# Four graph layers on one core: the hubs' weighted values summed over places by identity products on TensorE

## Chip, core and metric

The kernel runs on one core of a Trainium2 chip. The metric is the device time of one execution in microseconds (us). A core has TensorE (PE), VectorE (DVE), ScalarE (ACT), GpSimd (POOL) and DMA queues, one of them issued by SyncE (SP). Each engine takes its instructions from its own queue in order, and engines wait for one another by semaphores. PE reads SBUF and writes PSUM.

## What is computed

Sixteen graphs of 1024 nodes with 64 channels go through four layers, each with a residual and a layer norm:

```python
x = _layernorm(x + _L0_gnn_ref(x, adj, nodemask, ...), axis=-1)   # quantiles over neighbours, then an MLP
x = _layernorm(x + _L1_gnn_ref(x, adj, ...), axis=-1)             # adj @ (x W)
x = _layernorm(x + _L2_gnn_ref(x, adj, ...), axis=-1)             # attention plus adj
x = _layernorm(x + _L3_gnn_ref(x, adj, nodemask, ...), axis=-1)   # quantiles over neighbours, then an MLP
```

The first and the last take, for every node and channel, the values of its neighbours (some edges are dropped by a rule of rank), sort them, and add the quantiles at 0.25, 0.5 and 0.75 with weights 0.25, 0.5 and 0.25, interpolated between two places:

```python
pos = jnp.clip(tau * (mf - 1.0), 0.0)
q = gather(lo) * (1.0 - frac) + gather(hi) * frac
agg = agg + wt * q
```

That is the same as a weighted sum of the sorted list over its places, where at most six weights of a list are not zero. The kernel computes it so.

## The kernel before

**Layers.** The two quantile layers of each of 16 batches make 32 "layers" (n = 0 to 31), worked in a pipeline. Seven streams are generators that yield instructions: graph (adjacency, dilation, ranks of nodes by degree, lists of neighbours), turn, pick, weight, middle (MLP, layer norms, the two middle layers), sort and fetch. The nodes are ordered by degree. The 128 with the longest lists are the hubs; the others are "short" and are sorted in three groups.

**The hubs' path of one layer.** The fetch stream issues 50 indirect DMAs on POOL that gather neighbours' rows into hrows (8 buffers of two gathers each). The turn stream (from L1488) transposes each with an identity product on PE into the PSUM tile "turned" (one buffer), and ACT copies from there into two SBUF tiles cols[0] and cols[1], each 128 partitions x 32 places x 55 columns (half a list's chunk in each column, channels on partitions). The sort stream runs long_lists (from L1616) on DVE: a network over the 32 places of each column, merges of columns, each step from cols to a spare tile or back. Then summed (L1673) multiplies a block by the fp16 weights hw and adds the 32 places by five halving additions (16, 8, 4, 2, 1 places), and small operations add the columns that belong to one list into tot. An event "block" says that a block is done, "hubdone" that both are. The turn stream waits for hubdone, turns tot with two products, ACT copies the result to hagg, and POOL puts it into DRAM. Only then does the turn stream begin the next layer's transposes.

A few columns of block 0 (the first SPLIT = 9) hold two half lists; there the upper 16 places are summed apart into "more" and added to another list's total.

**The short rows' path.** 85 gathers a layer on POOL into rows, a network on DVE, a weighting on ACT, sums over places by identity products on PE ("picked"), and puts.

**Order of the instructions.** give_out (L259) decides it while the program is built. It keeps a planned time for each engine and tile, takes from the heads of all streams the instruction that could start first (the earlier stream when equal), and puts it at the end of its engine's queue. The costs come from Queue.times (L214): a cost, in which the engine is held, and a lateness until others see the result. Every instruction so placed is recorded by one closure, so the profile gives nearly all of them line L211, and groups are told apart by tiles and shapes. A Wait in a stream holds the stream in the plan only; on the chip waits come from the tiles that are read and written.

Of the kernel before, what the change touches and what calls it, by code (L numbers as in the profile page):

```python
# [9 lines left out]
F32 = mybir.dt.float32  # L10
# [7 lines left out]
ALU = mybir.AluOpType  # L18
AX = mybir.AxisListType
# [19 lines left out]
HC = 55  # L39
# [3 lines left out]
HUB_RUNS = ((0, 18, 9, 32, 1, False), (9, 10, 25, 0, 1, False), (34, 10, 8, 32, 1, False), (42, 35, 13, 0, 1, False),  # L43
            (55, 0, 1, 0, 8, True), (63, 1, 1, 0, 5, True), (68, 2, 2, 0, 4, True), (76, 4, 6, 0, 2, True),
            (88, 4, 6, 64, 1, True), (94, 48, 16, 0, 1, True))
# [13 lines left out]
SPLIT = 9  # L59
UPPER = (0, 27, SPLIT, 16, 1, False)  # L60
CH = 32
# [125 lines left out]
class Queue:  # L187
# [26 lines left out]
    def times(self, name, args, sizes, halves, psum, accum):  # L214
        n, half = max(sizes), all(halves)
        if self.engine == "V":
            rate = 1.9 if name == "tensor_reduce" and n > 256 and not psum else 1.1
            if name in ("tensor_tensor", "tensor_mul", "tensor_add", "tensor_sub") and half and not psum:
                rate = 0.52
            elif name in ("tensor_scalar", "tensor_copy", "memset") and not psum:  # L220
                rate = 0.26 if half else 0.52
            return 75 + rate * n, 120
        if name == "dma_start":
            return 100, 3000 + 128 * sizes[0] * 4 / 100.0
        if self.engine == "A":
            return 110 + 1.0 * sizes[0] + 200 * accum, 150
        if self.engine == "T":
            cols = sizes[0]
            if halves[1]:
                return max(45, 0.5 * cols), 250  # L230
            return (220 if name == "transpose" else 2 * max(200, 1.25 * cols)), 250
        if self.engine == "G":
            return (1435, 4000) if name == "indirect_dma_start" else (1000, 200)
        raise ValueError(name)
# [601 lines left out]
def listed_path(ctx: ExitStack, tc: tile.TileContext, x, adj, nodemask,  # L836
# [5 lines left out]
    P = 128  # L842
# [7 lines left out]
    V, A, T, G = nc.vector, nc.scalar, nc.tensor, nc.gpsimd  # L850
# [10 lines left out]
    ident = const.tile([P, P], F32, name="ident")  # L861
# [12 lines left out]
    run = const.tile([P, P], F16, name="run")  # L874
# [52 lines left out]
    for (first, places), (end, fewer) in zip(HUB_CAPS, HUB_CAPS[1:] + ((64, 0),)):  # L927
        more = const.tile([P, 1], F32, name=f"more{first}")
# [5 lines left out]
    for k in (1, 2, 3):  # L934
        s = const.tile([P, 7, MOST], F32, name=f"shifted{k}")
# [56 lines left out]
    with tc.tile_pool(name="wps", bufs=2, space=PSUM) as wps:  # L992
        pt = wps.tile([C, C], F32, name="pt")
# [18 lines left out]
    qp = pool("qp")  # L1012
    small = {"g": pool("small_g", 2), "t": pool("small_t", 2)}
    psm = pool("psm", space=PSUM)
    psh = pool("psh", space=PSUM)
# [11 lines left out]
    V, A, T, G, D = (Queue(c, e) for c, e in zip("VATGD", (nc.vector, nc.scalar, nc.tensor, nc.gpsimd, nc.sync)))  # L1027
    events = set()
# [459 lines left out]
    def turn_stream():  # L1488
        for n, (l, b) in enumerate(layers):
            k = batches[b]  # L1490
            yield Wait("hidx", b)
            k.cols = [None, None]
            for g in range(0, NG, 4):
                pt = psh.tile([P, 4 * P], F32, name="turned")
                for i in range(g, min(g + 4, NG)):
                    yield Wait("h", n, i)
                    yield T.transpose(pt[:, (i - g) * P:(i - g + 1) * P], k.hrows[i].rearrange("p h c -> p (h c)"),
                                      ident).after(6000)
                events.add(("turned", n, g // 4))
                first, end = g * GC, min((g + 4) * GC, GW)  # L1500
                by_slot = pt.rearrange("p (c s) -> p s c", s=CH)
                for i in range(2):
                    c0, c1 = max(first, i * GB), min(end, (i + 1) * GB)
                    if c0 < c1 and c0 == i * GB:
                        if n:
                            yield Wait("block", n - 1, i)
                        k.cols[i] = qp.tile([P, CH, HC], F32, name=f"cols{i}")
                        for c, m, s0, places in EMPTY:
                            if c // HC == i:
                                yield A.copy(k.cols[i][:, s0:s0 + places, c - i * HC:c - i * HC + m],  # L1510
                                             bigs[:, :places * m].rearrange("p (s c) -> p s c", c=m))
                    if c0 < c1:
                        runs = [(0, CH, c, n_ * chunks, to, 0) for c, _, n_, _, chunks, to in WHOLE]
                        runs += [(q * PART, PART, c, n_, to, s0) for q, c, n_, _, _, to, s0 in PARTS]
                        for at, places, c, m, to, s0 in joined(runs):
                            a, b = max(c0, c), min(c1, c + m)
                            if a < b:
                                d = to + a - c - i * HC
                                yield A.copy(k.cols[i][:, s0:s0 + places, d:d + b - a],
                                             by_slot[:, at:at + places, a - first:b - first])  # L1520
                    if c0 < c1 and c1 == (i + 1) * GB:
                        events.add(("cols", n, i))
            yield Wait("hubdone", n)
            pt = psh.tile([P, C], F32, name="turned")
            for h in range(2):
                rs = slice(h * C, (h + 1) * C)
                yield T.matmul(pt[rs], k.tot[rs], ident[rs, rs], start=True, stop=True)
            k.hagg = qp.tile([P, C], F32, name="hagg", bufs=2)
            yield A.copy(k.hagg, pt)
            events.add(("hagg", n))  # L1530
# [23 lines left out]
    def sort_stream():  # L1554
        for n, (l, b) in enumerate(layers):
            k = batches[b]
            yield Wait("cols", n, 0)
            if n > 1:
                yield Wait("put", n - 2)
            k.tot = qp.tile([P, 64], F32, name="tot", bufs=2)  # L1560
            yield from long_lists(n, k)
            events.add(("hubdone", n))
            for q, (t0, ntiles, places) in enumerate(TILE_GROUPS):
                yield Wait("rows", n, q)
                for t, s, m in PAIRS:
                    if t0 - 1 <= t < t0 - 1 + ntiles:
                        yield V.memset(k.rows[l, q][P // 2:, s:s + 2 * m, t - t0 + 1, :], BIG)
                yield from network((k.rows[l, q], spare((places, ntiles, C))), plans[q], C)
                events.add(("net", n, q))
# [46 lines left out]
    def long_lists(n, k):  # L1616
# [56 lines left out]
        def summed(block, spans):  # L1673

            yield Wait("hw", n, block)
            w = bufs[side[spans[0][0]]][block]
            for c0, c1 in spans:
                assert len(set(side[c0:c1])) == 1
                cols = slice(c0 % HC, c0 % HC + c1 - c0)
                yield V.tensor_tensor(w[:, :, cols], bufs[side[c0]][block][:, :, cols], k.hw[block][:, :, cols], ALU.mult)  # L1680
            half = CH // 2
            skip = 0 if block else SPLIT
            while half:
                yield V.tensor_add(w[:, :half, skip:], w[:, :half, skip:], w[:, half:2 * half, skip:])
                half //= 2
                skip = 0
            for c0, first, lists, p0, chunks, by_list in sorted(HUB_RUNS, key=lambda run: run[3]):
                if c0 // HC == block:
                    v = w[:, 0, c0 % HC:c0 % HC + lists * chunks]
                    v = v.rearrange("p (l k) -> p l k" if by_list else "p (k l) -> p l k", k=chunks)  # L1690
                    mine = k.tot[:, first:first + lists]
                    if p0:
                        yield V.tensor_add(mine, mine, v[:, :, 0])
                    elif chunks == 1:
                        yield V.tensor_copy(mine, v[:, :, 0])
                    elif chunks == 2:
                        yield V.tensor_add(mine, v[:, :, 0], v[:, :, 1])
                    else:
                        yield V.tensor_reduce(mine, v, AX.X, ALU.add)
            if not block:  # L1700
                more = qp.tile([P, SPLIT - 1], F32, name="more")
                yield V.tensor_reduce(more, w[:, CH // 2:, :SPLIT - 1].rearrange("p s c -> p c s"), AX.X, ALU.add)
                mine = k.tot[:, UPPER[1]:UPPER[1] + SPLIT - 1]
                yield V.tensor_add(mine, mine, more)
            events.add(("block", n, block))

        yield from first(0)

# [243 lines left out]
```

## Time and profile before

| what | value |
|---|---|
| median of 3 runs | 7255.36 us (7244.06 to 7256.55) |
| the profiled execution | 7250.51 us, its span 7248.6 us |
| granted TensorE clock, mean | 0.646 |
| POOL gathers and puts | 4544, mean 1.1 us, with about 0.3 us of issue between two |
| DVE: hub sort steps, spare<-cols | 1792 instructions, 1016.1 us |
| DVE: hub sort steps, cols<-spare | 1632 instructions, 1017.1 us |
| PE: picked (sums over places of short rows) | 432.1 us of 832 products from rows |
| PE waiting for tot ("turned <- DVE tot") | 236.3 us in 17 waits, longest 80.5 |

Busy time is what the engine's own records cover; times of waits are idle times of an engine, put down to what ended them last. A group's line gives busy time, mean time of one and the idle time before it. On PE instructions overlap in the pipeline, so that the busy time over the count tells what one more costs, and the mean of one tells how long it is under way. Where stretches are given, they run from the span's start.

### The profile page before, as it was taken

How to read it: one execution, taken by the hardware profiler on the slowest of the kernel's cores; microseconds unless marked ns; L12 is line 12 of the kernel's file. 1: busy time of each engine (PE TensorE's matmuls, PEld its weight loads, DVE VectorE, ACT ScalarE, POOL GpSimd, SP SyncE). 2: the span in 40 equal slices, each digit the busy share in tenths (PEclk: the TensorE clock that was granted, in tenths of full speed). 3: DMA queues.
4: the chain of work that ended last, by engine and by line, in shares of the span. 5: the costliest groups of instructions: out<-in, count | busy, mean ns of one | idle time of the engine just before them, and what ended most of it. 6: DMA issues, size and time to landing. Idle time of an engine off the chain costs nothing. (4 is left out here: it accounts for less than half of the span.)

```text
span 7248.6 us, 75571 instructions
## 1 busy us (share of the span) xinstructions
PE 4032.2 (56%) x20163; PEld 2014.5 (28%) x20163; DVE 6433.9 (89%) x16469; ACT 2468.9 (34%) x8066; POOL 5144.3 (71%) x4606
## 2 busy tenths in 40 slices
PE   4358664847475564646647465574756647262541
PEld 3223232323232322223223232322223223121211
DVE  4878798999999999989989899898989989999876
ACT  3324333343333434234342333423234342222231
POOL 2653777777776777767777776777767677777764
PEclk7557676757566665766666566665666766565565
DMA  2231413141323223231231322323231232121211
GB/s 68 68 100 34 127 35 107 52 113 50 87 64 88 61 58 85 68 88 49 59 102 53 88 57 66 86 56 89 68 87 49 59 99 56 45 71 42 57 41 23
DMA packets 515446, 498.74 MB, mean 69 GB/s; under 512 B 203712, under 2 KB 351424, under 8 KB 514752
## 3 DMA queue, kind: packets, MB, share of 16 engines
q1 hardware_dynamic: 218048, 262.03, 11.9%
q0 software_dynamic: 146432, 150.24, 9.5%
q10 hardware_dynamic: 150528, 81.54, 3.8%
q8 instruction: 164, 2.69, 0.1%
q14 instruction: 274, 2.24, 0.1%
HBM read 393.02 MB, written 102.50 MB: 68 GB/s over the span
## 5 line engine op out<-in xcount | busy, mean ns | idle before, releaser
L211 POOL DMA_INDIRECT rows<-table,idx x2720 | 3064.2, 1127 | 829.9 <-issue 790.6
L211 POOL DMA_INDIRECT hrows<-table,hidx x1600 | 1781.5, 1113 | 905.1 <-issue 373.3
L211 DVE TENSOR_TENSOR spare<-cols 128x192 f32<-128x192 f32 (+15 forms) x1792 | 1016.1, 599 | 57.4 <-ACT cols L211 40.5
L211 DVE TENSOR_TENSOR cols<-spare 128x528 f32<-128x528 f32 (+14 forms) x1632 | 1017.1, 652 | 11.1
L211 PE MATMUL picked<-rows,ident 128*128 128x512 f32 (+5 forms) x832 | 432.1, 628 | 399.8 <-ACT rows L211 375.9
L211 ACT ACTIVATE rows<-rows,wt 128x64 f32<-128x64 f32 x1856 | 499.3, 348 | 207.8 <-DVE rows L211 183.6
L211 DVE TENSOR_TENSOR spare<-rows 128x128 f32<-128x128 f32 (+8 forms) x1056 | 539.2, 541 | 31.7 <-DMA rows<-table,idx 17.8
L211 POOL DMA_INDIRECT sums<-agg,node x224 | 256.1, 1143 | 313.9 <-ACT agg L211 213.0
L211 DVE TENSOR_TENSOR rows<-spare 128x512 f32<-128x512 f32 (+8 forms) x864 | 451.0, 551 | 1.9
L211 PE MATMUL two<-ident,a 128*128 128x128 f32 x1024 | 239.6, 411 | 364.9 <-DMA a<-in_adj_dram 271.7
L211 DVE TENSOR_TENSOR spare<-spare 128x64 f32<-128x64 f32 (+11 forms) x640 | 399.4, 624 | 16.5
L211 PE MATMUL one<-xt,wt 64*128 64x512 f32 x512 | 374.1, 1024 | 36.1 <-DVE top L211 35.6
L211 ACT ACTIVATE v<-two,before 128x128 f16<-128x128 f32 x1024 | 278.8, 385 | 310.7 <-DVE before L211 179.4
L211 PE MATMUL pi<-hot,numbers 128*32 128x200 f16 x4096 | 241.5, 327 | 250.9 <-DVE hot L211 248.6
L211 DVE TENSOR_TENSOR rows<-rows,spare 128x128 f32<-128x128 f32 (+4 forms) x1088 | 347.6, 328 | 17.5
L211 PE MATMUL po<-at,y 128*64 128x512 f32 x512 | 285.2, 752 | 138.0 <-DMA at<-adjt 94.7
L211 PE MATMUL turned<-ident,hrows 128*128 128x128 f32 x800 | 229.7, 358 | 228.6 <-DMA hrows<-table,hidx 209.2
L211 PE MATMUL po<-at,x 128*64 128x512 f32 x512 | 277.5, 780 | 129.6 <-DMA at<-adjt 117.9
L211 PE MATMUL pu<-e,x 128*65 128x512 f32 x512 | 311.0, 698 | 62.3 <-ACT e L211 62.3
L211 ACT COPY at<-two 128x1024 f32<-128x1024 f32 x128 | 129.5, 1012 | 612.7 <-PE two L211 562.0
L211 PEld LDWEIGHTS picked<-rows,ident 128*128 128x128 f32 x832 | 182.5, 272 | 523.7 <-ACT rows L211 487.7
L211 DVE TENSOR_SCALAR hot<-slot 128x1600 f16<-128x1600 f16 x512 | 300.4, 590 | 25.1 <-PE pi L211 22.8
(273 smaller groups left out, 9052.7 us busy)
## 6 DMA issues: line engine op xcount, KB each, us to landing
at<-adjt SPq DMA_DIRECT2D x512, 256.0 KB
a<-in_adj_dram SPq DMA_DIRECT2D x128, 512.0 KB
adjt<-at ACTq DMA_DIRECT2D x128, 512.0 KB
rows<-table,idx POOLq DMA_INDIRECT x2720
hw<-hwt SPq DMA_DIRECT2D x64, 440.0 KB
hrows<-table,hidx POOLq DMA_INDIRECT x1600
hwt<-ho ACTq DMA_DIRECT2D x64, 220.0 KB
ag<-sums SPq DMA_DIRECT2D x32, 256.0 KB
```

The lines of the kernel that those rows point to most:

```text
L211: return Step(lambda: f(*args, **kw), self.engine, cost, late, reads, writes, "dma" in name)
```

## The change

The five halving additions of each block leave summed. It now only multiplies, always into cols, and gives an event "weighed". The turn stream waits for it and adds the places on PE: 32 products of the fp32 identity with the 55 columns of one place each, all into one PSUM tile; for the last 16 places of block 0 the first 9 columns are left out. The small operations that make tot stay on DVE, but read PSUM and stand in the turn stream; a sum of two columns is a reduction now. "more" is reduced from cols as before. Beside that, the planner's costs for ACT and PE are changed.

```diff
         if self.engine == "A":
-            return 110 + 1.0 * sizes[0] + 200 * accum, 150
+            first = 60 if name == "copy" else 180
+            return first + 0.82 * sizes[0] + 100 * accum, 150
         if self.engine == "T":
             cols = sizes[0]
             if halves[1]:
-                return max(45, 0.5 * cols), 250
-            return (220 if name == "transpose" else 2 * max(200, 1.25 * cols)), 250
+                return max(45, (0.3 if args[0].shape[0] <= 32 else 0.85) * cols), 250
+            return max(170, 240 if name == "transpose" else 1.4 * cols), 250
...
-            yield Wait("hubdone", n)
+            k.tot = qp.tile([P, 64], F32, name="tot", bufs=2)
+            for block in range(2):
+                yield Wait("weighed", n, block)
+                w = k.cols[block]
+                pt = psh.tile([P, HC], F32, name="turned")
+                for s in range(CH):
+                    skip = 0 if block or s < CH // 2 else SPLIT
+                    yield T.matmul(pt[:, skip:], ident, w[:, s, skip:], start=(s == 0), stop=(s == CH - 1))
+                for c0, first, lists, p0, chunks, by_list in sorted(HUB_RUNS, key=lambda run: run[3]):
+                    if c0 // HC == block:
+                        v = pt[:, c0 % HC:c0 % HC + lists * chunks]
...
+                        if p0:
+                            yield V.tensor_add(mine, mine, v[:, :, 0])
+                        elif chunks == 1:
+                            yield V.tensor_copy(mine, v[:, :, 0])
+                        else:
+                            yield V.tensor_reduce(mine, v, AX.X, ALU.add)
...
+                events.add(("block", n, block))
...
             yield Wait("hw", n, block)
-            w = bufs[side[spans[0][0]]][block]
+            w = k.cols[block]
...
-            half = CH // 2
-            skip = 0 if block else SPLIT
-            while half:
-                yield V.tensor_add(w[:, :half, skip:], w[:, :half, skip:], w[:, half:2 * half, skip:])
-                half //= 2
-                skip = 0
...
-            events.add(("block", n, block))
+            events.add(("weighed", n, block))
```

Two more lines go: in the sort stream, layer n no longer waits in the plan for the puts of layer n - 2 before tot is made, and hubdone is gone.

More of the change, by code (lines that the diff above doesn't have):

```diff
@@ L1522, in turn_stream @@
                         events.add(("cols", n, i))
-            yield Wait("hubdone", n)
+            k.tot = qp.tile([P, 64], F32, name="tot", bufs=2)
[9 more added lines that the diff above has]
+                        v = pt[:, c0 % HC:c0 % HC + lists * chunks]
+                        v = v.rearrange("p (l k) -> p l k" if by_list else "p (k l) -> p l k", k=chunks)
+                        mine = k.tot[:, first:first + lists]
+                        if p0:
[4 more added lines that the diff above has]
+                            yield V.tensor_reduce(mine, v, AX.X, ALU.add)
+                if not block:
+                    more = qp.tile([P, SPLIT - 1], F32, name="more")
+                    yield V.tensor_reduce(more, w[:, CH // 2:, :SPLIT - 1].rearrange("p s c -> p c s"), AX.X, ALU.add)
+                    mine = k.tot[:, UPPER[1]:UPPER[1] + SPLIT - 1]
+                    yield V.tensor_add(mine, mine, more)
+                events.add(("block", n, block))
             pt = psh.tile([P, C], F32, name="turned")
@@ L1557, in sort_stream @@
             yield Wait("cols", n, 0)
-            if n > 1:
-                yield Wait("put", n - 2)
-            k.tot = qp.tile([P, 64], F32, name="tot", bufs=2)
             yield from long_lists(n, k)
-            events.add(("hubdone", n))
             for q, (t0, ntiles, places) in enumerate(TILE_GROUPS):
@@ L1680, in summed @@
                 yield V.tensor_tensor(w[:, :, cols], bufs[side[c0]][block][:, :, cols], k.hw[block][:, :, cols], ALU.mult)
-            half = CH // 2
-            skip = 0 if block else SPLIT
-            while half:
-                yield V.tensor_add(w[:, :half, skip:], w[:, :half, skip:], w[:, half:2 * half, skip:])
-                half //= 2
-                skip = 0
[L1687 to L1704, printed above, removed]
-            events.add(("block", n, block))
+            events.add(("weighed", n, block))
         yield from first(0)
```

## Prediction

> **What bounds the kernel now.** First the page's busy rows. Two engines are nearly full: VectorE (DVE) by busy time, and GpSimd (POOL), whose 4544 gathers and puts have gaps between them that no busy row counts.
>
> ```profile
> span 7248.6 us, 75571 instructions
> PE 4032.2 (56%) x20163; PEld 2014.5 (28%) x20163; DVE 6433.9 (89%) x16469; ACT 2468.9 (34%) x8066; POOL 5144.3 (71%) x4606
> ```
>
> Then the stretches, because start and end are chains of single waits. I cut where the hub fetches of the fifth layer and of the last one begin. Columns: stretch, its length, busy time of PE, PEld, DVE, ACT, POOL with counts, granted clock, DMA.
>
> ```profile
> 0.00:1146.00 1146.00, 645.11 (x4063) 335.19 (x4063) 889.69 (x2482) 396.72 (x1184) 628.43 (x595) 0.67 0.26 71
> 1146.00:6967.00 5821.00, 3328.82 (x15920) 1647.94 (x15920) 5371.09 (x13598) 2015.54 (x6655) 4351.60 (x3861) 0.65 0.26 70
> 6967.00:7249.00 282.00, 58.27 (x180) 31.34 (x180) 173.15 (x392) 56.64 (x230) 164.23 (x151) 0.54 0.12 26
> ```
>
> In the middle stretch DVE works 5371 of 5821 us (92%). Who waited for whom there, on POOL and then on DVE (us in total, times, longest us):
>
> ```profile
> POOL rows L211 <- issue: 666.3, 2183, 0.8
> POOL hrows L211 <- issue: 318.5, 1045, 0.3
> POOL hrows L211 <- PE turned L211: 260.4, 54, 27.8
> POOL sums L211 <- issue: 58.0, 179, 2.3
> ```
> ```profile
> DVE near L211 <- ACT at L211: 137.2, 14, 16.8
> DVE top L211 <- PE one L211: 56.3, 71, 3.5
> DVE gone L211 <- ACT v L211: 21.7, 37, 1.5
> ```
>
> POOL's own work is 4352 + 666 + 319 + 58 = 5395 us. The one large wait it has is for "turned", the transposes that free the fetch buffers of the hubs, 260 us. Those stand in the turn stream behind the hub sums of the layer before, and the sums behind DVE's sort. An example from POOL's timeline: it resumes at 4412.66 after 25.28 us, and the timeline of "turned" has the copy of the finished hub sums (hagg) at 4402.1 and the next layer's first transposes from 4411.1. So DVE sets the pace and POOL waits for it, with at most 260 us (4.5% of the stretch) to gain before POOL itself is the bound. TensorE (PE) is idle 44% of the span, but it is one in-order queue and often blocked.
>
> **What goes from DVE.** The timeline of DVE shows one layer's removed additions. Block 1, at 2662.35, has all five in a row:
>
> ```profile
> 2661.63 0.69 DVE L211 TENSOR_TENSOR spare<-cols,hw 128x512 f32<-128x512 f32 x1
> 2662.35 2.71 DVE L211 TENSOR_TENSOR spare<-spare 128x880 f32<-128x880 f32 x5
> 2665.09 0.29 DVE L211 TENSOR_REDUCE tot<-spare 128x1 f32<-128x8 f32 x3
> ```
>
> Block 0, in layer 0, has its own between operations of the graph stream:
>
> ```profile
> 234.99 1.58 DVE L211 TENSOR_TENSOR cols<-cols 128x736 f32<-128x736 f32 x2
> 236.49 0.69 DVE L211 TENSOR_SCALAR near<-at 128x1024 f16<-128x1024 f32 x1
> 237.09 0.38 DVE L211 TENSOR_TENSOR cols<-cols 128x220 f32<-128x220 f32 x1
> 237.39 0.22 DVE L211 TENSOR_TENSOR near<-near,noteye 128x128 f16<-128x128 f16 x1
> 237.52 0.52 DVE L211 TENSOR_TENSOR cols<-cols 128x110 f32<-128x110 f32 x2
> ```
>
> Block 1: 2.71 us. Block 0: 1.58 + 0.38 + 0.52 = 2.48 us. Together 5.19 us a layer, times 32 layers = **166 us off DVE**. The products with the weights stay, in number and size; they now always write into cols.
>
> **What comes on PE.** 64 products a layer, each the 128x128 fp32 identity against 55 fp32 columns (46 for the last 16 of block 0). The nearest row is the same identity against 64 columns, in eights:
>
> ```profile
> L211 PE MATMUL picked<-side,ident 128*128 128x64 f32 x512 | 87.4, 320 | 7.6 <-ACT side L211 7.6
> ```
>
> The 320 ns overlap one another; what each adds is 87.4/512 = 171 ns. Another row with 64 columns and 128 rows, "one<-w,ht", gives 112.9/512 = 221 ns; on the timeline sixteen products of "one<-l2gs" take 1.90 us, 119 ns each. I take 171 ns as for 64 columns: 64 x 171 = 10.9 us a layer, 350 us in all (bounds 244 and 453). PE goes from 4032 to about 4380 us, 60% of the span. That is not on the path by itself; what matters is the burst of 32 x 171 = 5.5 us (3.8 to 7.1) between the last weighted product and the small sums.
>
> The clock stands behind that spread. The page's slices show a granted clock from 0.5 to 0.7 with means of 0.54 to 0.67 in the three stretches, and the same shape takes 119 or 221 ns. The Trainium skill (TensorE: Matmul & The Clock Gate, "Why this matters for your kernels") says that an idle gap of more than some 3 us between bursts puts TensorE back to half clock. The trace's spread fits, and by that rule alone, a burst that always follows a wait for DVE would always run slow. By the rule every burst would cost the upper bound, 1.6 us more than I take; by the row it costs the mean. I stay with the row, since PE has other work around the bursts.
>
> **The tail.** Twelve small operations a layer that write tot or more stay on DVE, one of them as a reduction instead of an addition (its neighbours: 0.29 us for three). Ten now read PSUM. The nearest row that reads PSUM, "slot<-two" 128x32, is 218 ns; "tot<-cols" copies from SBUF have a median of 179 ns. 10 x 32 x 0.04 us = 13 us more (bounds 0 and 30).
>
> **The new wait.** The tail waits for PE twice a layer, 64 times, where before DVE waited for nothing. Behind it on DVE's queue are the sort of the next block, the networks of the short rows and the graph's operations, so a late PE stops everything. Below: 0, if the planner always finds 5.5 us of other DVE work, which it has, since sorting goes on. Rows: "top<-one" is 256 reductions straight behind a PE product and lost 65.5 us in the whole run, 0.26 us each; at the other end PE, when it is itself blocked by ACT on "picked", loses 375.9 us in 100 waits, 3.8 us each. I take 0.5 us, twice the first row because the burst is 32 instructions that others can split: 64 x 0.5 = 32 us (bounds 0 and 243).
>
> **Chain.** In layer 0 block 1 takes 313.33 - 307.31 = 6.0 us from its first weighted product to hagg. The 2.75 us of additions become 5.5 us of products and a few tenths of semaphores, so hagg comes about 3 us later after its product, while block 0 gives 2.5 us back ahead of it. So where the chain alone decides (layers 0 to 3 and 31) I count nothing. hw buffers, the cols of block 1 and tot are held some us longer; the next layer's copies into cols stand in the same turn stream behind hagg anyway, so that costs nothing beyond the above.
>
> **Order estimates.** They change no instruction, but the order of all queues. The trace shows the old ones wrong both ways: a 64-column fp32 product was planned at 400 ns (171 traced) and a 512-column one at 1280 (608 for "pu<-e,x", 311.0/512), a 128-column f16 one at 64 (124.3/1024 = 121). The new ones give 170, 717 and 109. PE no longer looks nearly full to the planner, so DVE operations that use PE's results are planned earlier, with less spare time. The waits of DVE in the middle stretch are the price on both sides: the three rows above are 215 us. Half of them gone is -110, half as many again +110. I take 0, as nothing in the trace tells the sign, and keep both ends.
>
> **Sum.** DVE gets 166 - 13 - 32 = 121 us. Of 32 layers 27 lie in the middle stretch, where DVE sets the pace: 121 x 27/32 = 102 us. POOL would then wait some 160 us instead of 260, and as the two meet more often I take off a fifth: **-82 us**. The profiled execution took 7250.5 us around its span of 7248.6, 4.9 below the median of the runs, 7255.4. 7250.5 - 82 = 7168, and with the step to the median about **7172 us**, 1.1% less.
>
> **Rivals.**
> (1) PE's queue becomes DVE's brake. Each of the 64 bursts waits in order behind some product that itself waits, and DVE stands. Price: 64 x w; from w = (166 - 13)/64 = 2.4 us on the change loses. For it: PE's 3.8 us per wait on "picked", and the new estimates that leave less spare time. Against: the waits of DVE on PE in the trace are 0.26 us in the mean and 3.5 at most on "top". With w = 3.8: 243 - 153 = +90, **7345 us**. Chance 0.28.
> (2) The change does what it says, and nothing follows: the path from one hagg to the next is latency (product, burst, tail, transposes, gathers), 3 us longer and 2.5 us shorter, and POOL's 260 us stay. For it: POOL is already at 5395 of 5821 us. Against: DVE never waits for cols in the middle stretch but once, so it is load, not latency. **7255 us**. Chance 0.08.
> (3) The better estimates also take half of DVE's waits, and the whole 121 us count: 7255 - 121 - 110 = **7025 us**. For it: the old errors of a factor of two. Against: POOL would need nearly all of its 260 us. Chance 0.08.
>
> **How the numbers follow.** The forecast has 0.56; its own range is 7090 (no stall, nothing lost to POOL, 121 us + 32 and a little order) to 7240. A measurement of this kernel tells about 0.2% (15 us) from no change: faster 0.56 + 0.08 = 0.64, within 0.08, slower 0.28. The range leaves out about half of rival 1 and most of rival 3: 7070 to 7340.
>
> **What would show it.** Right: DVE's busy time near 6285 us with 320 instructions fewer and no "cols<-cols" halvings; PE's near 4380 with 2048 products more; DVE's wait for "turned" under 60 us; POOL's wait for "turned" near 160. Wrong: DVE waiting for "turned" over 150 us (rival 1), "hrows" still waiting 260 us with DVE less busy (rival 2), or DVE's waits for at, one and v moved by more than 100 us (the order).

## The result, and the profile after

The changed kernel takes 7564.5 us (7554.8 to 7583.8), the kernel before 7252.1 beside it: 1.0435 times, 95% interval 1.041 to 1.046. It is **slower by 312 us**; forecast was 7172. The profiled execution took 7554.8 us around a span of 7553.0.

The page's first lines of the changed kernel:

```profile
span 7553.0 us, 83637 instructions
PE 4660.3 (62%) x24259; PEld 2772.8 (37%) x24259; DVE 6276.5 (83%) x16149; ACT 2496.2 (33%) x8066; POOL 5080.9 (67%) x4606
```

DVE's busy time fell by 157 us, as forecast, and the span rose by 304. So DVE's idle time, span less busy, rose from 815 to 1277 us. And PE has 4096 records more, for 2048 products. Who DVE waited for, and then POOL:

```profile
DVE tot L211 <- PE turned L211: 379.4, 62, 8.5
DVE near L211 <- ACT at L211: 189.1, 32, 14.5
DVE top L211 <- PE one L211: 114.2, 107, 4.4
DVE rs L211 <- PE one L211: 65.7, 14, 7.4
```
```profile
POOL hrows L211 <- PE turned L211: 658.7, 98, 50.2
```

The same waits in the kernel before, over its whole span:

```profile
DVE near L211 <- ACT at L211: 199.7, 33, 16.8
DVE top L211 <- PE one L211: 65.5, 79, 3.5
DVE rs L211 <- PE one L211: 6.7, 5, 3.1
```
```profile
POOL hrows L211 <- PE turned L211: 273.9, 59, 27.8
```

DVE's wait for "turned" is new: 62 waits, with 64 bursts in the run. "top" has nearly doubled and "rs" grown from 6.7 to 65.7: operations that the change doesn't touch. POOL's wait went up from 274 to 659 us instead of down.

The timeline shows one burst (the 32 products of a block), block 1 of a layer in the middle (start, length, what, count, idle before it; some lines left out):

```profile
4594.66 0.69 DVE L211 TENSOR_TENSOR cols<-cols,hw 128x512 f32<-128x512 f32 x1
4595.40 13.90 PE L211 MATMUL turned<-cols,ident 128*128 128x55 f32 x64 [23.73 <-DVE cols L211]
4595.46 0.27 DVE L211 MEMSET rows<- 64x256 f32 x1
...
4601.33 0.68 DVE L211 TENSOR_TENSOR ag<-ag,xn 128x512 f32<-128x512 f32 x1
4609.34 0.38 DVE L211 TENSOR_REDUCE tot<-turned 128x1 f32<-128x8 f32 x4 [7.33 <-PE turned L211]
```

The 32 products are 64 records of 217 ns, 13.9 us (a record is one line that the profile keeps of an instruction). The planner had put 6.5 us of other work (4595.46 to 4602.0) between the weighting and the tail on DVE, about what 32 x 170 ns plus the latenesses comes to. That ran out, and DVE stood for 7.33 us.

### The profile page after: what moved, and what is told of

It reads as the page before. It is cut to its first block, busy times and chain, and to the rows that moved or that the text cites. A ratio compares the mean times of both kernels' runs of the same rounds, so it can differ in the third digit from the quotient of the medians.

```text
span 7553.0 us, 83637 instructions
## 1 busy us (share of the span) xinstructions
PE 4660.3 (62%) x24259; PEld 2772.8 (37%) x24259; DVE 6276.5 (83%) x16149; ACT 2496.2 (33%) x8066; POOL 5080.9 (67%) x4606
## 5 line engine op out<-in xcount | busy, mean ns | idle before, releaser
L211 POOL DMA_INDIRECT hrows<-table,hidx x1600 | 1729.5, 1081 | 1282.6 <-PE turned L211 658.7
L211 PE MATMUL turned<-cols,ident 128*128 128x55 f32 (+1 forms) x4096 | 834.9, 399 | 562.9 <-DVE cols L211 562.9
L211 DVE TENSOR_TENSOR spare<-cols 128x192 f32<-128x192 f32 (+15 forms) x1792 | 1013.8, 599 | 69.8 <-ACT cols L211 51.7
L211 PEld LDWEIGHTS turned<-cols,ident 128*128 128x128 f32 x4096 | 830.5, 311 | 595.2 <-DVE cols L211 399.6
L211 DVE TENSOR_TENSOR cols<-spare 128x528 f32<-128x528 f32 (+14 forms) x1632 | 1011.8, 652 | 12.5
L211 PE MATMUL picked<-rows,ident 128*128 128x512 f32 (+5 forms) x832 | 406.0, 599 | 261.6 <-ACT rows L211 253.1
L211 PE MATMUL turned<-ident,hrows 128*128 128x128 f32 x800 | 257.3, 385 | 217.0 <-DMA hrows<-table,hidx 171.3
L211 DVE TENSOR_TENSOR spare<-spare 128x64 f32<-128x64 f32 (+7 forms) x480 | 316.2, 659 | 10.6
L211 PEld LDWEIGHTS picked<-rows,ident 128*128 128x128 f32 x832 | 165.1, 250 | 433.2 <-ACT rows L211 358.8
L211 ACT COPY cols<-turned 128x64 f32<-128x64 f32 (+12 forms) x864 | 168.2, 300 | 458.9 <-PE turned L211 451.2
L211 PE MATMUL one<-xt,wt 64*128 64x512 f32 x512 | 291.6, 893 | 39.1 <-DVE top L211 38.6
```

Of the source, the lines that this page charges most:

```text
L211: return Step(lambda: f(*args, **kw), self.engine, cost, late, reads, writes, "dma" in name)
```

## The experiments

Three theories were set against each other. **A**: the burst is planned at 5.4 us and takes 13 or more, so the tails stand too early in DVE's queue. **B**: the burst is on the path from one hagg to the next layer's transposes, and its length costs the time. **C**: the new costs alone make a bad order.

### New sums with the old costs (e1)

```diff
         if self.engine == "A":
-            first = 60 if name == "copy" else 180
-            return first + 0.82 * sizes[0] + 100 * accum, 150
+            return 110 + 1.0 * sizes[0] + 200 * accum, 150
...
-                return max(45, (0.3 if args[0].shape[0] <= 32 else 0.85) * cols), 250
-            return max(170, 240 if name == "transpose" else 1.4 * cols), 250
+                return max(45, 0.5 * cols), 250
+            return (220 if name == "transpose" else 2 * max(200, 1.25 * cols)), 250
```

> The new sums by identity products, with the planner's old costs for ACT and PE. Theory A (the burst of 32 products takes 13 us, the new cost of 170 ns plans 5.4, so the small sums stand too early in DVE's queue and DVE stands still): the old cost of 400 ns plans 12.8 us, so DVE's wait for turned falls from 379 us to under 120 us and the time to 7150-7300 us. Theory B (the burst lies on the path from one hagg to the next layer's transposes, 12 us a layer, and DVE's idle time only follows from that): POOL's wait for turned stays over 550 us and the time at 7500-7600. Theory C (the new costs alone make the order worse): under 7250.

Measured: 7042.5 us, 0.9719 of before (0.9694 to 0.9744): **2.8% faster than before**, and below what A said. The waits fell as A said; the time alone would also fit C, so that e2 has to decide between the two. Its page and its waits:

```profile
span 7043.5 us, 83543 instructions
PE 4660.1 (66%) x24259; PEld 2717.9 (39%) x24259; DVE 6277.1 (89%) x16149; ACT 2458.7 (35%) x8066; POOL 5140.7 (73%) x4606
```
```profile
DVE top L211 <- PE one L211: 65.2, 117, 1.8
DVE tot L211 <- PE turned L211: 22.2, 35, 2.7
POOL hrows L211 <- PE turned L211: 77.9, 56, 13.5
```

PE and DVE do the same work as in the changed kernel to within 1 us; only the order differs, and 510 us with it. A burst of block 0 there, with DVE's weighting and tail:

```profile
2711.48 1.99 DVE L211 TENSOR_TENSOR cols<-cols,hw 128x1760 f32<-128x1760 f32 x1
2713.53 2.81 PE L211 MATMUL turned<-cols,ident 128*128 128x55 f32 x12 [0.20 <-DVE cols L211]
2716.54 6.90 PE L211 MATMUL turned<-cols,ident 128*128 128x55 f32 x32
2723.60 4.34 PE L211 MATMUL turned<-cols,ident 128*128 128x46 f32 x20
2727.98 0.26 DVE L211 COPY tot<-turned 128x25 f32<-128x25 f32 x2 [0.54 <-PE turned L211]
```

The burst is as long as before, 14.4 us, but DVE comes to the tail 0.54 us early instead of 7.33. From the last weighting of a layer to its hagg this kernel needs about 23 us (16 to 26 over the layers), the changed one 11 to 32, mostly 18, the kernel before 4 to 10. So the longer path is no price by itself: **B is refuted** by a kernel that is faster than both although its path is longer, and whose POOL waits 78 us where B asked for over 550.

### Old sums with the new costs (e2)

The same lines the other way round, in the kernel before.

> The kernel before, sums by halving additions, with only the planner's costs changed. Theories A and B: the costs alone are worth within 1% of the kernel before, 7180-7325 us, DVE's waits for one together within 60 us of before. Theory C: at least 7400 us, with over 100 us more of DVE's waits for at, one and v.

Measured: 7204.3 us, 0.9939 (0.9919 to 0.996). C, which asked for 7400 us or more, falls: by themselves the costs gain 0.6%. But DVE's waits for "one" were not within 60 us of before: "top" went from 65.5 to 113.9 and "rs" from 6.7 to 58.7 us, while "near" fell from 199.7 to 92.0. The sums with old costs give -203 us, the costs alone -41, both together +312: the two belong together badly.

### The burst's true length told (e3)

```diff
-                    yield T.matmul(pt[:, skip:], ident, w[:, s, skip:], start=(s == 0), stop=(s == CH - 1))
+                    step = T.matmul(pt[:, skip:], ident, w[:, s, skip:], start=(s == 0), stop=(s == CH - 1))
+                    step.cost = 430
+                    yield step
```

> The changed kernel, except that the planner is told 430 ns for each of the hubs' products (64 records of 217 ns were traced in a burst of 32). Nothing else of the costs changes. Theory A: DVE's wait for turned under 100 us, 7250 us or less. Theory B: that wait falls too, but the burst stays in the path: mult to hagg stays at 17 us or more, POOL waits over 500 us for turned, at least 7450 us.

Measured: 7264.2 us, 1.0024 (1.0012 to 1.0036).

```profile
DVE near L211 <- ACT at L211: 151.2, 27, 16.1
DVE top L211 <- PE one L211: 127.7, 134, 2.8
DVE hot L211 <- PE pi L211: 51.9, 26, 9.5
DVE tot L211 <- PE turned L211: 14.4, 21, 1.8
```

DVE's wait for "turned" is 14.4 us, and one number in the plan is worth 300 of the 312 us: that is A, shown. POOL waits 340 us, not B's 500 and more. But it ends 14 us over A's mark and 222 above e1, though the burst is about right in both. What is left lies in the other costs or in the luck of an order, since e3 and e1 differ in nothing else; e3's DVE is idle for 997 us, e1's for 766.

### Wide products (e4)

```diff
-                pt = psh.tile([P, HC], F32, name="turned")
-                for s in range(CH):
+                pw = psh.tile([P, 8, HC], F32, name="turned")
+                for s in range(0, CH, 8):
                     skip = 0 if block or s < CH // 2 else SPLIT
-                    yield T.matmul(pt[:, skip:], ident, w[:, s, skip:], start=(s == 0), stop=(s == CH - 1))
+                    yield T.matmul(pw[:, :, skip:], ident, w[:, s:s + 8, skip:], start=(s == 0), stop=(s == CH - 8))
+                pt = qp.tile([P, HC], F32, name="eighth")
+                yield V.tensor_reduce(pt, pw.rearrange("p s c -> p c s"), AX.X, ALU.add)
```

> The changed kernel, but four products a block of eight places (440 columns) instead of 32 of one place, and DVE reduces the eight places that are left from PSUM. The 55-column products are bound by loading the identity (213 ns a record at half clock, against 46 to 92 of columns): eight records of 440 columns should take 3 to 6 us a block instead of 13.7, and the reduction about 0.6 us of DVE. Theories A and B: DVE's wait for turned under 130 us, POOL's under 350, 7100-7280 us. Theory C: 7350 us or more.

Measured: 7180.9 us, 0.9906 (0.9885 to 0.9926), with the changed kernel's costs.

```profile
3101.76 1.46 DVE L211 TENSOR_TENSOR cols<-spare,hw 128x1248 f32<-128x1248 f32 x1
...
3106.53 4.25 PE L211 MATMUL turned<-cols,ident 128*128 128x440 f32 x8
3110.82 0.62 DVE L211 TENSOR_REDUCE eighth<-turned 128x55 f32<-128x440 f32 x1 [3.17 <-PE turned L211]
```
```profile
DVE eighth L211 <- PE turned L211: 101.4, 43, 7.5
```

Four products of 440 columns take 4.25 us here (2.90 in another block), the 32 of 55 columns 13.9, though the columns are the same 1760. A part of that is the clock: it was granted at 0.75 in the mean here, at 1.00 in the block of 2.90 us and at 0.50 in the burst of 13.9. The rest is not: at the same clock a record of 440 columns takes a little over three times one of 55 (last section), and not eight times. So the small products are bound by something other than columns. DVE's wait for the burst is 101 us in 43 waits instead of 379: A again, by a shorter burst instead of a longer plan. B had named the same marks, and POOL's 271 us lie within them too, so this run doesn't part the two.

### What the other costs do

Theory **A2**: an fp32 product that is no transpose leaves two records, as the 64 records of 32 products show, so 1.4 x columns is the cost of half a product, for all fp32 products. Theory **D**: e1 fell on a lucky order. In all runs from here on the kernel before itself took 8960 to 9390 us, as it seems because the engines got their instructions late (last section); they can be compared among themselves, as ratios, and not with e1 to e4. The kernels of e5 to e8 were run more than once; e17 is e1's kernel and e18 the changed one.

```diff
-            return max(170, 240 if name == "transpose" else 1.4 * cols), 250
+            return (240 if name == "transpose" else 2 * max(170, 1.4 * cols)), 250
```

is the kernel with two records; the three others are the wide products with all old costs, the new sums with new ACT and old PE costs, and the new sums with new PE and old ACT costs.

> Four wide products a block (as in e4), with the old costs for ACT and PE. Theory A2 (the new PE costs are those of one record, where an fp32 product leaves two, so all fp32 work and not the burst alone is planned at half its length; that costs what e3 did not win back): as e1 or better, 6950-7060 us. Theory D (e1 fell on a lucky order; near plans scatter by 100 us and more): anywhere from 7000 to 7250.

> The changed kernel with one change in the costs: an fp32 product that is no transpose is planned at two records, 2 x max(170, 1.4 x columns). f16, transposes and ACT keep the new costs. Theory A2: 7000-7120 us, DVE's wait for turned under 60 us, its wait for one (top) near 65 us instead of 114. Theory D: anywhere from 7000 to 7264 (e3).

> The changed kernel with the old PE costs and the new ACT costs. Theory A2: the ACT costs are not the harm, within 1% of e1, 6970-7110 us. Theory D: anywhere from 7000 to 7250.

> The changed kernel with the new PE costs and the old ACT costs. Theory A2: the PE costs are the whole harm, 7450-7650 us, DVE's wait for turned over 250 us. Theory D: over 7250 us too, since the burst is still planned at 5.4 us; so this run is against A2 alone if it is under 7400.

> The kernel of e5 again, beside a kernel before that is not itself disturbed (in e5's call it took 8964 us). Theory A2: 6950-7060 us. Theory D: anywhere from 7000 to 7250.

> The kernel of e6 again for the same reason: an fp32 product is planned at two records, all else as in the changed kernel. Theory A2: 7000-7120 us. Theory D: anywhere from 7000 to 7264.

> The kernel of e7 again for the same reason: new sums, old PE costs, new ACT costs. Theory A2: 6970-7110 us. Theory D: anywhere from 7000 to 7250.

> The kernel of e8 again for the same reason: new sums, new PE costs, old ACT costs. Theory A2: 7450-7650 us, with DVE's wait for turned over 250 us; under 7400 speaks against it.

> The kernel of e6 beside an undisturbed kernel before: an fp32 product is planned at two records, all else as in the changed kernel. Theory A2 (halved fp32 costs are the rest of the harm): 7000-7120 us, DVE's wait for turned under 60 us. Theory D (orders scatter): anywhere from 7000 to 7264.

> The kernel of e8 beside an undisturbed kernel before: new sums, new PE costs, old ACT costs. Theory A2: 7450-7650 us with DVE's wait for turned over 250 us. Under 7400 speaks against it.

> The kernel of e5 beside an undisturbed kernel before: four wide products a block and the old costs. If the burst's length still costs something in a good order: 6950-7020 us. If not (DVE waits for nothing in e1 and only loses 35 us of reductions): 7040-7110 us.

> The kernel of e6 once more: an fp32 product is planned at two records, all else as in the changed kernel. Beside a kernel before of 7250 us, theory A2 (halved fp32 costs outside the hubs are the rest of the harm): 7000-7120 us, DVE's wait for turned under 60 us. Theory D (orders scatter): anywhere from 7000 to 7264.

> The kernel of e1, beside a kernel before that gets its instructions late. Theory A2: it is well below the two-record kernel's ratio only if costs besides the fp32 ones matter; A2 says as the two-record kernel, 1.01-1.03 of before, and DVE's wait for turned under 60 us. If all the old costs matter (ACT and f16 too): 0.97-1.00. If late instructions eat the gain of the products themselves, since 8192 more of PE's instructions have to be brought: over 1.00 whatever the costs, and the wide products' 0.975 is due to their fewer instructions.

> The changed kernel, beside a kernel before that gets its instructions late. Theories A and A2: as the kernel with the new PE costs, 1.09-1.12 of before, since the ACT costs are not the harm, with DVE's wait for turned over 250 us. Theory D: 1.02-1.08.

| sums | costs | ratio to before (95%) | DVE top <- PE one, us | DVE's wait for the burst (tot or eighth <- PE turned), us |
|---|---|---|---|---|
| 32 products | all old (e17) | 1.021 (1.010 to 1.033) | 81 | 22 |
| 32 products | new, fp32 at two records (e6, e10, e13, e16) | 1.019, 1.010, 1.033, 1.024 | 74 (e6), 65 (e10), 75 (e13) | 129, 105, 246 |
| 32 products | ACT new, PE old (e7, e11) | 1.036, 1.036 | – | – |
| 32 products | PE new, ACT old (e8, e12, e14) | 1.101, 1.109, 1.107 | 132 (e12), 179 (e14) | 294, 425 |
| 32 products | all new, the changed kernel (e18) | 1.102 (1.085 to 1.119) | 147 | 296 |
| 4 products | all old (e5, e15) | 0.976, 0.973 | 74 (e5), 42 (e15) | 8.5, 12.5 |

The intervals of the repeated ones reach 0.7 to 1.9% to either side. e9, the wide products again, was 8895.2 us beside 8959.7, without an interval.

In these runs the kernels with 32 products fall into two groups. With PE costs that count a product as one record, whatever ACT's costs, the ratio is 1.10 to 1.11; with the old PE costs or with two records it is 1.01 to 1.04. That is for A2 and against D: the two-record line alone brings the changed kernel to the old costs' ratio, and e18's interval lies above D's 1.02 to 1.08. New ACT costs with old PE costs, at 1.036, can't be told from 1.021, so a per cent or so may be theirs.

Four things speak less clearly. The two-record line also lengthens the plan of the burst, from 5.4 to 10.9 us, so it doesn't part A, the burst, from A2's other products; e3, which does, has no run beside these. DVE's wait for the burst was to be under 60 us with two records and was 105 to 246: the old cost plans 12.8 us, and the burst takes 13.9 even with instructions in time. The table's last columns hold only what the profile names: all idle time of DVE before "tot" is 566 us in e17 and 559 in e18 and doesn't tell them apart, while before "top" it is 230 to 390 us with the old PE costs or two records and 630 to 740 with the new ones. And the absolute times that were expected were missed by all, since before was not at 7250.

In e1 to e4 the same two groups show in "top": 65 us with the old PE costs (before and e1), 111 to 128 with the new ones (after, e2, e3, e4). What stays open is how much of the 222 us between e3 and e1 the two-record line would win back where instructions come in time, and how far orders scatter by luck there; neither was measured.

The wide products with the old costs are the only version below before where instructions come late. Where they come in time, the best measured is e1; the wide products with old costs have no such run.

## Why the prediction was wrong, point by point

- **DVE's saving: right in its sum.** 166 - 13 us were forecast, 157 measured (6433.9 to 6276.5), with 320 instructions fewer. The halvings were worth 160, and reading PSUM cost nothing: the ten operations a layer that read the sums took 51.7 us in the changed kernel and 54.7 before, so that two small errors offset each other.
- **"64 x 171 = 10.9 us a layer, 350 us in all": here it failed.** The 171 ns were 87.4 us over 512 records. But pick_stream issues eight such products a layer, 256 in all, so a product is two records, and costs 342. The count in that line was there to be held against the code. The bounds have the same slip (the "sixteen products" at 119 ns are sixteen records), and the 832 "products from rows" in the table of the kernel before are 832 records too. Measured were 4096 records at 834.9/4096 = 204 ns, 408 ns a product and 835 us in all: twice 171 from the count, and a fifth more from a lower clock.

```profile
L211 PE MATMUL turned<-cols,ident 128*128 128x55 f32 x3072 | 624.5, 395 | 562.9 <-DVE cols L211 562.9
```

- **The burst:** "5.5 us (3.8 to 7.1)" was 13.9 behind an idle stretch of 23.7 us.
- **The new wait: this is where the time went.** 0.5 us a time was 379.4/64 = 5.9, above even the end of 3.8. The step said that the planner always finds 5.5 us of other DVE work. It did, 6.5 us in the burst shown, but the burst took 13.9. The wait's size is not that of an average wait on PE; it is what the real burst is longer than the planned one. The planned 170 ns and the 171 of the row agreed because both were of one record. Rival 1 had the mechanism (PE as DVE's brake) and the point (2.4 us) right, and its price too low: 379 - 157 = +222 us against +90. The other 82 us of the span's 304 are waits at other operations: "top", "rs" and "hot" took 128 us more, and others a little less.
- **The order estimates:** I wrote that the old costs were wrong by a factor of two for fp32. They were near: 400 against 342 to 408 for a small product, 1280 against 2 x 607 = 1215 for 512 columns (311.0/512 a record). The new ones were wrong. The value of 0 was fair for the costs alone (e2: -41 us), but I added the terms, and these two don't add: with the new sums the same costs are worth 312 + 203 = 515 us. As I read it, halved costs hurt most where a consumer is put straight behind a producer, which is what the new sums add.
- **The chain:** hagg comes 12 us later after its weighting instead of 3. It is no price (e1). POOL's wait, forecast at 160 us in the middle stretch, is 635 there in the changed kernel (659 over the span), and 78 over the whole span in e1: it follows DVE.
- **The kernel that the forecast describes** is nearest to e1. The saving of 157 us with no new waits gives 7252 - 157 = 7095; it made 7042, as DVE's idle time also fell by 48 us. That is below the prediction's 7090 to 7240: the fifth taken off for POOL was not lost there, since POOL's wait fell to 78 us.

The rule on the clock: the burst at 4595.40 came behind 23.73 us of idle PE and took 217 ns a record throughout, at a granted clock of 0.50 (columns as in the prediction's table of stretches, the clock third from the end):

```profile
4595.40:4609.30 13.90, 13.90 (x65) 13.80 (x65) 6.32 (x10) 0.00 (x0) 0.00 (x0) 0.50 0.11 33
```

Of the gaps between the starts of successive records in the changed kernel a tenth are 112 ns or less, and the median is 213; the first are those at full clock, the second those at half. The Trainium skill (TensorE: Matmul & The Clock Gate, "What's actually happening") has TensorE at half clock by default and again after an idle window of about 3.4 us, and full clock after as long a busy one. This case agrees, but for the end of it: 13.9 us of unbroken small products did not bring the full clock back, and 44 of the 64 bursts ran at half clock from end to end. In one burst the clock even fell while small products ran with hardly a pause:

```profile
1292.77 6.76 PE L211 MATMUL turned<-cols,ident 128*128 128x55 f32 x58
```
```profile
1292.80:1299.30 6.50, 6.50 (x58) 6.50 (x59) 6.40 (x10) 2.15 (x8) 4.46 (x5) 0.99 0.51 146
1299.40:1301.00 1.60, 1.60 (x11) 1.24 (x9) 0.47 (x1) 0.05 (x1) 1.32 (x1) 0.50 0.03 6
```

With the wide products of e4, 42 of the 64 bursts began at half clock and came to full clock before they ended. The prediction had set the rule aside in favour of the row's mean, which mixes both clocks; for a record the upper bound was the better value.

## What to carry to other kernels

Before a mean from a profile becomes a cost, hold the group's count against the number that the code issues: one fp32 product was two records, and the slip halved both the estimate and the planner's costs. Where an order is written from costs, moving work to another engine adds a wait whose price is the difference between the planned and the real time of the producer, so test the move with the costs left alone and the costs alone. And here one wide product was far cheaper than many narrow ones with the same columns.

## What was not expected of the hardware

**Narrow fp32 products don't get cheaper with fewer columns.** From start to start, fp32 records of 46, 55, 64 and 128 columns against the 128 x 128 identity all have a median of 112 ns at full granted clock and of 213 at half; those of 440 columns (e4) have 369 and 734. The means are mixtures of the two: 64 columns gave 171 ns a record before, 55 and 46 together 204, 46 alone 216.9/1024 = 212. So below some 128 columns there is a floor. Each record carries its own load of the 128 columns of the identity, which the profile has in equal number (x24259); that the load sets the floor is the likely reason, but no run shows it by itself. The Trainium skill (TensorE: Matmul & The Clock Gate, "LDWEIGHTS (loading the stationary operand)") gives a load as its columns over 1.2 ns, an estimate of 107 ns for 128 columns. The records at full clock, 112 ns, are near it; those at half clock take twice that, and most of the new products ran there.

**Instructions can come late.** In e5 to e18 PE had stretches in which it got an instruction only every 1.4 us or so, with nothing else to wait for that the profile shows ("issue"). From e12's timeline of PE and its weight loads:

```profile
303.91 0.10 PEld L211 LDWEIGHTS <-near 128*128 128x128 f16 x1 [2.69 <-issue]
305.31 0.17 PE L211 MATMUL one<-later,near 128*128 128x9 f16 x1 [2.63 <-issue]
306.71 0.10 PEld L211 LDWEIGHTS <-near 128*128 128x128 f16 x1 [2.69 <-issue]
308.11 0.17 PE L211 MATMUL one<-later,near 128*128 128x9 f16 x1 [2.63 <-issue]
```

Instructions that ran took as long as elsewhere (DVE busy 6291.5 us in e18), but the kernel before took 24 to 30% longer. DVE's idle time for which the profile names no cause is 1915 us in e18, and 18 in the changed kernel of the first runs; that it is the supply of instructions is a reading of this, not a measurement. There the number of instructions itself seems to cost: the 32 products with old costs lose 2.1% where they otherwise gain 2.8, and the wide ones, with 7100 instructions fewer (76436 against 83543), gain 2.4 to 2.7%. Why the instructions came late was not found out.
